# Reordering the opening of a fused Mamba, MLP and mixture-of-experts kernel on one core: when blocks are normalised, when their router logits are made, and when the scan begins

## The chip, the cores and the metric

The kernel runs on one core of one Trainium2 chip. A core has a matrix engine (TensorE, PE in the profile, with its weight loads as PEld), VectorE (DVE), ScalarE (ACT), GpSimd (POOL) and SyncE (SP), which here issues nearly all direct transfers. Each engine works its own list of instructions in the order in which the program names them. The metric is device time in microseconds; before the change it is 1587.38 us (median of three runs, 1585.76 to 1589.98).

## The reference

The input is x, 4096 tokens (2 sequences of 2048) of 256 channels. Cut to what matters:

```
xn = layernorm(x)
# branch s: a Mamba block, then an MLP, each with a residual
r  = rmsnorm(xn)
xp, z = split(r @ in_proj.T)                  # 512 channels each
xc = silu(conv4(xp) + conv_b)
dt, B, C = from xc @ x_proj.T                 # dt = softplus(. @ dt_proj.T + b); 16 states
h_t = h_(t-1) * exp(dt_t * A) + dt_t * xc_t * B_t      # 512 channels x 16 states
y  = (sum_state h_t * C_t + xc * D) * silu(z)
x1 = xn + y @ out_proj.T
s  = x1 + silu(rmsnorm(x1) @ mlp_w1.T) @ mlp_w2.T
# branch g: 8 experts, the best 2 of each token
w  = softmax(xn @ gate_w + gate_b); top 2
g  = silu(sum over the 2 of  w * (relu(xn @ w1[e]) @ w2[e]))
out = x + s * g
```

## The kernel before

Tokens are cut into 8 blocks of 512 (NBLK); a block is four tiles of 128 tokens (J), and blocks are gated in pairs (GB is 2, four groups). The work falls into an opening, a long scan loop and a short ending.

**The opening** (lines 1099 to 1155). For a block b, `moments(b)` takes mean and variance of its four tiles on VectorE (L247, L248). `factors(b0, b1)` turns them into scales and offsets for a range of blocks in one go, 16 small VectorE instructions and four ScalarE ones that alternate (L253 to L265, L234, L235). `norm(b)` has ScalarE write the doubly normalised tile xr (L274) and TensorE transpose it into two PSUM banks (L288): the pair of `ps_b` for an even block, the banks "du" and "y" for an odd one, and for blocks 6 and 7 (EARLY is 6) two of the three banks "h". `logits(b)` copies the transposes to SBUF as xrT (L295), stores xrT (L299), makes router logits on TensorE (L302), and then, in the same function, turns x into its layer norm in place on ScalarE (L309) and stores it (L315). `gate(g)` picks the best two experts for two blocks: some 15 VectorE instructions (L399 to L421), two counting products on TensorE (L415, L418), and 13 more on VectorE (L422 to L438). `scatter_group(g)` then has GpSimd write the rows of those two blocks to the lists of their experts in DRAM: 16 indirect transfers (L456), each a full layer-normed tile. In between stands `front(0)`, a generator: four channel projections of block 0 (L554) with convolution taps on VectorE (L579) and SiLU (L593), the small projection (L599), and the steps dt (L618, `exps` L626 to L632, `log_v` L640, sums L645 and L646). `go(n)` advances it by n pieces. `load_bc` fetches B or C of one pair of states from DRAM, spread over all partitions (L695, 512 KB each). B and C tiles lie in the places in which the opening keeps x (blocks 0 to 5, tags B0 to B5) and xrT (blocks 2 to 7, tags C2 to C7), so a load waits for the last reader of what lies there, and SyncE's later transfers wait behind it.

**The order of evictions.** A product is put on TensorE at once, but the work on its result is put in a list, `later`, with a due time; `tick()` in the opening, and every half step of the scan, moves the time by one and issues what is due.

**The scan loop** (L1311) has 256 steps n: 8 blocks, 4 channel groups d, 8 pairs g of states. A step is one product on VectorE (L1334) and two scans (L1338), with two exponentials on ScalarE (L1228) issued LEAD (2) steps ahead; GpSimd multiplies by C (L1269) and from step 8 on adds the pair (L1271), and TensorE sums over states (L1241) LAG (3) steps later. After each half step, `draw` issues about 2 us of other TensorE work (HALF), each piece counted at the price that its generator yields, from the first list that has some: `pre`, `zs` (gate projections, L705), `projs` (output projections, L759), `chain` (the rest of `front(0)`, then `front(c+1)`), and `side`, all the feed-forward work: 39 expert tiles of 256 tokens, then 16 MLP tiles, each 64 TensorE instructions (L851, L863). A generator that yields "wait" gives up its turn for that half step. `side` is passed over while `pre` holds anything.

`pre` is `routed()`: for blocks 6 and 7 `norm`, `logits` and the last two loads of C; then `gate(3)`, 16 scatters four at a time, `tiles_of_experts()` (a table of which expert owns which tile, some 25 VectorE instructions, L483 to L531), `fill_up()` (eight transfers, L537), and the loads of the first expert. In `side`, the first expert waits four more half steps and then is transposed (L841). Counted out by these rules, the transposes of the first expert tile stand in the program at the first half of step 9.

Of the kernel before, what the change touches and what calls it, by code (L numbers as in the profile page):

```python
# [10 lines left out]
AF = mybir.ActivationFunctionType  # L11
ALU = mybir.AluOpType
# [37 lines left out]
def kernel(  # L50
# [58 lines left out]
    def x_of(b, j):  # L109
        per = J // len(xts[b])  # L110
        return xts[b][j // per][:, j % per, :]
# [128 lines left out]

    stat = rows.tile([P, 8, NI], F32, tag="x1", name="stat")
    mv = stat[:, 0:2, :].rearrange("p a i -> p (a i)").rearrange("p (i a) -> p i a", a=2)
    pts, banks_of = {}, {}
    def moments(b):
        st = hpool.tile([P, J, nc.vector.BN_STATS_DIM], F32, tag="hid", name=f"st{b}")
        for j in range(J):
            nc.vector.bn_stats(st[:, j, :], x_of(b, j))  # L247
            nc.vector.bn_aggr(mv[:, b * J + j, :], st[:, j, :])  # L248

    def factors(b0, b1):  # L250
        i = slice(b0 * J, b1 * J)
        var, rstd, tmp0, ms, r_all, off = (stat[:, 2 + n, i] for n in range(6))
        nc.vector.tensor_scalar_add(var, mv[:, i, 1], LN_EPS)  # L253
        rsqrt(rstd, var, tmp0)

        nc.vector.tensor_mul(ms, rstd, rstd)
        nc.vector.tensor_mul(ms, ms, mv[:, i, 1])
        nc.vector.tensor_scalar_add(ms, ms, RMS_EPS)
        rsqrt(r_all, ms, tmp0)
        nc.vector.tensor_mul(unr[:, i], ms, r_all)  # L260

        nc.vector.tensor_mul(tmp0, rstd, r_all)
        nc.vector.scalar_tensor_tensor(off, mv[:, i, 0], -1.0, tmp0, ALU.mult, ALU.mult)

        nc.vector.scalar_tensor_tensor(var, mv[:, i, 0], -1.0, rstd, ALU.mult, ALU.mult)  # L265
# [4 lines left out]
    def norm(b):  # L270
        xr = work.tile([P, J, DM], F32, tag="h", name=f"xr{b}")
        for j in range(J):
            i = b * J + j
            nc.scalar.activation(  # L274
                xr[:, j, :], x_of(b, j), AF.Identity,
                scale=both_norms[:, i : i + 1], bias=off[:, i : i + 1],
            )
        if b >= EARLY:
            pt, ns = zip(*(bank("h", [P, T], f"pt{b}_{k}") for k in range(KM)))
            banks_of[b] = ns  # L280
        elif b % 2:
            pt = [ps_1.tile([P, T], F32, tag=tag, name=f"pt{b}_{tag}") for tag in ("du", "y")]
        else:
            both = ps_b.tile([P, KM, T], F32, tag="b", name=f"pt{b}")
            pt = [both[:, k, :] for k in range(KM)]
        for k in range(KM):
            for j in range(J):
                nc.tensor.transpose(pt[k][:, ts(j, P)], xr[:, j, ts(k, P)], ident)  # L288
        pts[b] = pt

    def logits(b):
        pool, tag = (bcp, f"C{b}") if b > 1 else (rows, "xrT")
        xrT[b] = pool.tile([P, KM, T], F32, tag=tag, name=f"xrT{b}")
        for k in range(KM):
            nc.scalar.copy(xrT[b][:, k, :], pts[b][k])  # L295
            if b in banks_of:
                drop(*banks_of[b][k])
        if b > 1:
            nc.sync.dma_start(xrd[b], xrT[b])  # L299
        for j in range(J):  # L300
            for k in range(KM):
                nc.tensor.matmul(  # L302
                    lgp[:, b * J + j, :], xrT[b][:, k, ts(j, P)], gw_sb[:, k, :],
                    start=(k == 0), stop=(k == KM - 1),
                )

        for j in range(J):
            i = b * J + j
            nc.scalar.activation(  # L309
                x_of(b, j), x_of(b, j), AF.Identity,  # L310
                scale=rstd[:, i : i + 1], bias=moff[:, i : i + 1],
            )
        per = J // len(xts[b])
        for k, xn in enumerate(xts[b]):
            nc.sync.dma_start(xnd[b][:, ts(k, per), :], xn)  # L315
# [47 lines left out]
    def drop(tag, n):  # L363
        gone.setdefault(tag, set()).add(n)
# [11 lines left out]
    def bank(tag, shape, name):  # L376
        n = ring(tag, 3 if tag == "h" else 1)
        pool = ps_h if tag == "h" else ps_1
        return pool.tile(shape, F32, tag=tag, name=name), n
# [717 lines left out]
        later.run()  # L1097

    later.at_once = False
    for b in range(GB):  # L1100
        moments(b)
    factors(0, GB)
    for b in range(GB):
        norm(b)
        for a in range(GB + 3 * b, GB + 3 * (b + 1)):
            moments(a)
    for b in range(GB):
        logits(b)
    ffns = [Expert(i) for i in range(NTILE)] + [
        Mlp(c, hf) for c in range(NBLK) for hf in range(2)  # L1110
    ]
# [2 lines left out]
    def go(pieces):  # L1114

        for _ in range(pieces):
            next(first)

    go(1)
    go(3)  # L1120
    go(3)
    tick()
    factors(GB, NBLK)
    gate(0)
    scatter_group(0)
    tick()
    norm(2)
    go(3)
    norm(3)
    tick()  # L1130
    logits(2)
    logits(3)
    tick()
    gate(1)
    scatter_group(1)
    tick()
    norm(4)
    go(3)
    tick()
    norm(5)  # L1140
    logits(4)
    go(3)
    tick()
    logits(5)
    tick()
    go(4)
    tick()
    gate(2)
    scatter_group(2)
    assert 0 in bcd and (0, 1) in dt_made  # L1150
    for which, gs in (
        ("B", (0, 1, 6, 7)), ("C", (0, 1)), ("B", (2, 3)), ("C", (2, 3)), ("B", (4, 5)), ("C", (4, 5)),
    ):
        for g in gs:
            load_bc(0, g, which)

    def routed():

        for b in range(EARLY, NBLK):
            norm(b)  # L1160
            yield 4 * MM
            yield "wait"
            logits(b)
            load_bc(0, b, "C")
            yield 2 * MM
            yield "wait"
        gate(NBLK // GB - 1)
        yield "wait"
        for i in range(NI - GI, NI):
            for k in range(TOPK):  # L1170
                scatter(i, k)
            if i % 2:
                yield "wait"
        tiles_of_experts()
        fill_up()
        ffns[0].begin()
        for h in range(4):
            ffns[0].load_w1(h)
            ffns[0].load_w2(h)
        yield "wait"  # L1180
        probabilities()
        for _ in ffns[0].rows():
            pass
# [118 lines left out]
    HALF = 2.0  # L1302

    pre.append(routed())
    chain.append(first)
    side.append(all_ffn(None))
    for n in range(LEAD):
        for q in range(2):
# [1 line left out]
    owed = 0.0  # L1310
    for n in range(NS):  # L1311
        c, d, g = at[n]
        if d == 0 and g == 0 and c % CPB != CPB - 1:
            hs[c] = small.tile([P, ND, DS], F32, tag="hs", name=f"hs{c}")
        if d == 0 and g == 1:
            zs.extend(gate_z(c, k) for k in range(ND))
        if c + 1 < NBLK:
            if d == 0 and g == 1 and c:
                xrT[c + 1] = rows.tile([P, KM, T], F32, tag="xrT", name=f"xrTr{c + 1}")
                nc.sync.dma_start(xrT[c + 1], xrd[c + 1])  # L1320
            if d == 0 and g == (4 if c else 0):
                chain.append(front(c + 1))
        if c > 0 and d == 0 and g == 0:
            projs.append(out_proj(c - 1))
        for q in range(2):
            later.now += 1
            if q == 0:
                if g == 0:
                    assert (c, d) in dt_made
                    dus[c, d] = ps_1.tile([P, T], F32, tag="du", name=f"du{c}_{d}")  # L1330
                    nc.vector.tensor_tensor(dus[c, d], dts[c, d], xcs[c, d], ALU.mult)
                hts[n] = work.tile([P, 2, T], F32, tag="h", name=f"h{c}_{d}_{g}")
                inp = ps_b.tile([P, 2, T], F32, tag="b", name=f"b{c}_{d}_{g}")
                nc.vector.tensor_tensor(  # L1334
                    inp, dus[c, d].unsqueeze(1).to_broadcast([P, 2, T]),
                    bct[c, "B", g], ALU.mult,
                )
            nc.vector.tensor_tensor_scan(  # L1338
                hts[n][:, q, :], das[n][:, q, :], inp[:, q, :],
                0.0 if c % CPB == 0 else hs[c - 1][:, d, 2 * g + q : 2 * g + q + 1],  # L1340
                ALU.mult, ALU.add,
            )
            if q == 0 and n > 0:
                save(n - 1)
                times_c(n - 1)
            exps(n + LEAD, q)
            later.run()
            if q == 0 and n >= LAG:
                sums(n - LAG)
            if q == 0:  # L1350

                past = n - BACK
                if past >= 0 and at[past][1] == ND - 1 and at[past][0] + 1 < NBLK:
                    load_bc(at[past][0] + 1, at[past][2])
            owed = draw(HALF + owed)
# [67 lines left out]
```

## Time and profile before

| | before |
|---|---|
| median of three runs | 1587.38 us |
| the profiled execution's own time | 1574.88 us |
| its span, first to last instruction | 1573.2 us |
| first scan of the loop starts | 113.8 us |
| transposes of the first expert tile start | 192.2 us |
| last scan ends | 1513.6 us |
| busy over the span: PE, DVE, POOL, ACT | 1400.0, 1247.0, 1154.7, 924.3 us |

A profile row of a timeline reads: start, length, engine, line of the kernel, operation, written tile <- read tiles, shapes, and in brackets how long the engine sat idle before it and what released it. Rows with the same line that follow one another are merged (x4 means four of them). Rows of the view by stretches give, for each stretch of time, the busy time of PE, PEld, DVE, ACT and POOL with the number of instructions, then the granted TensorE clock (1.00 is full), the share of the DMA engines and GB/s. A busy PE at half clock does half the work.

### The profile page before, as it was taken

The numbers are of one execution on the slowest core, as the hardware profiler recorded it, in microseconds if no ns is written. First come the engines' busy times: TensorE is split into PE (matmuls) and PEld (weight loads), VectorE is DVE, ScalarE is ACT, GpSimd is POOL, SyncE is SP. The second block draws the span as 40 slices with busy tenths as digits, with TensorE's granted clock in tenths as the row PEclk, the third lists the DMA queues.
The fourth block names the chain that finished last, engine by engine and source line by source line (L and its number), as shares of the span: only waits on it lengthen the run. The fifth ranks groups of instructions, "written<-read, shape, count | busy, mean of one in ns | idle before, by whom it ended". The sixth has DMA issues, their size and how long they took to land. (4 is left out here: it accounts for less than half of the span.)

```text
span 1573.2 us, 18460 instructions
## 1 busy us (share of the span) xinstructions
PE 1400.0 (89%) x5246; PEld 982.6 (62%) x5246; DVE 1247.0 (79%) x1362; ACT 924.3 (59%) x1898; POOL 1154.7 (73%) x767
## 2 busy tenths in 40 slices
PE   4447499999999899999999999989899988899967
PEld 3324167765777577766776677657665656577736
DVE  5435898789788988799869976996689966899952
ACT  4365476566665776567647765676456764465423
POOL 1446768976887689878976888678966678678842
PEclk9556699999999999999999999999999988999988
DMA  5365534763477245924593459234863337636322
GB/s 178 111 239 194 176 100 141 246 231 99 134 237 268 84 130 179 342 84 132 174 339 89 127 168 333 91 117 132 276 215 95 100 101 246 235 121 192 103 97 84
DMA packets 203749, 265.17 MB, mean 169 GB/s; under 512 B 21744, under 2 KB 174192, under 8 KB 203648
## 3 DMA queue, kind: packets, MB, share of 16 engines
q1 hardware_dynamic: 197504, 247.21, 47.7%
q0 software_dynamic: 6144, 16.79, 3.2%
q8 instruction: 42, 0.69, 0.2%
q14 instruction: 59, 0.48, 0.1%
HBM read 227.50 MB, written 36.44 MB: 168 GB/s over the span
## 5 line engine op out<-in xcount | busy, mean ns | idle before, releaser
L1269 POOL TENSOR_TENSOR h<-h,C 128x1024 f32<-128x1024 f32 x256 | 610.1, 2385 | 211.1 <-ACT hs L1265 173.0
L1338 DVE TENSOR_TENSOR_SCAN h<-da,hs,b 128x512 f32<-128x512 f32 x384 | 478.9, 1271 | 32.9 <-PE y L1241 10.2
L1228 ACT ACTIVATE da<-dt,a_neg 128x512 f32<-128x512 f32 x512 | 359.4, 718 | 35.5 <-DVE h L1338 34.1
L1241 PE MATMUL y<-h,ident 128*128 128x512 f32 x594 | 308.3, 620 | 37.3 <-POOL h L1269 25.3
L1334 DVE TENSOR_TENSOR b<-du,B 128x1024 f32<-128x1024 f32 x256 | 314.8, 1230 | 6.2
L851 PE MATMUL phe<-xsTe,w_e 128*128 128x256 f32 x1248 | 288.4, 383 | 7.1 <-ACT hide L951 5.4
L1271 POOL TENSOR_TENSOR h<-h 128x512 f32<-128x512 f32 x215 | 279.1, 1298 | 16.8
L863 PE MATMUL poe<-w_e,hide 128*128 128x256 f32 x1248 | 289.8, 381 | 0.0
L851 PEld LDWEIGHTS phe<-xsTe,w_e 128*128 128x128 f32 x1248 | 238.6, 192 | 71.3 <-issue 26.3
L863 PEld LDWEIGHTS poe<-w_e,hide 128*128 128x128 f32 x1248 | 236.2, 191 | 66.6 <-issue 35.0
L951 ACT ACTIVATE hide<-phe,b 128x256 f32<-128x256 f32 x312 | 129.3, 469 | 128.8 <-PE phe L851 128.8
L1241 PEld LDWEIGHTS y<-h,ident 128*128 128x128 f32 x594 | 112.1, 197 | 129.6 <-issue 66.5
L1338 DVE TENSOR_TENSOR_SCAN h<-da,b 128x512 f32<-128x512 f32 x128 | 151.3, 1211 | 13.1 <-PE y L1241 3.2
L851 PE MATMUL phm<-xsTm,w_m 128*128 128x256 f32 x512 | 128.5, 406 | 13.9 <-DVE hidm L1012 10.4
L851 PEld LDWEIGHTS phm<-xsTm,w_m 128*128 128x128 f32 x512 | 104.0, 205 | 46.0 <-DVE hidm L1012 14.8
L456 POOL DMA_INDIRECT xs_d<-xt,slot x64 | 63.6, 993 | 88.3 <-issue 78.9
L863 PE MATMUL pom<-w_m,hidm 128*128 128x256 f32 x512 | 117.5, 381 | 1.7 <-DVE xom L1083 1.7
L863 PEld LDWEIGHTS pom<-w_m,hidm 128*128 128x128 f32 x512 | 97.6, 192 | 26.1 <-issue 10.3
L1039 POOL DMA_INDIRECT ykm<-ys_d,row_y x64 | 61.9, 967 | 40.5 <-issue 14.4
L1265 ACT COPY hs<-h 128x2 f32<-128x2 f32 x192 | 36.2, 188 | 94.2 <-DVE h L1338 78.0
L1010 ACT ACTIVATE hidm<-phm 128x512 f32<-128x512 f32 x64 | 37.9, 592 | 75.9 <-PE phm L851 65.5
L1012 DVE SCALAR_TENSOR_TENSOR hidm<-hidm,phm 128x512 f32<-128x512 f32 x64 | 42.8, 671 | 48.7 <-ACT hidm L1010 48.7
(174 smaller groups left out, 1463.2 us busy)
## 6 DMA issues: line engine op xcount, KB each, us to landing
w_e<-in_w SPq DMA_DIRECT2D x312, 256.0 KB
B<-bcd SPq DMA_DIRECT2D x64, 512.0 KB
C<-bcd SPq DMA_DIRECT2D x64, 512.0 KB
w_m<-in_mlp_w1T SPq DMA_DIRECT2D x64, 256.0 KB
w_m<-in_mlp_w2T SPq DMA_DIRECT2D x64, 256.0 KB
xs<-xs_d SPq DMA_DIRECT2D x39, 256.0 KB
ys_d<-ys SPq DMA_DIRECT2D x39, 256.0 KB
b<-in_b SPq DMA_DIRECT2D x39, 128.0 KB
```

Of the source, the lines that this page charges most:

```text
L456: r = nc.gpsimd.indirect_dma_start(out=xs_d, out_offset=bass.IndirectOffsetOnAxis(ap=slot[:, k, i : i + 1], axis=0), in_=x_of(i // J, i % ...
L851: nc.tensor.matmul(ph[:, q, :], self.w1[c0 // 2][:, k, ts(q, P)], self.xT[:, k, :], start=(k == 0), stop=(k == KM - 1),)
L863: nc.tensor.matmul(po[:, j, :], self.hid[c // 2][:, c % 2, ts(j, P)], self.w2[c // 2][:, c % 2, :], start=(c == 0 and j == 0), stop=(c == ...
L951: nc.scalar.activation(hc[:, q, :], ph[:, q, :], AF.Relu, bias=self.b1[:, c0 + q : c0 + q + 1])
L1012: lambda: nc.vector.scalar_tensor_tensor(hc, hc, 1.0, ph, ALU.add, ALU.mult), n
L1039: nc.gpsimd.indirect_dma_start(out=yk[k][:, j, :], out_offset=None, in_=ys_d, in_offset=bass.IndirectOffsetOnAxis(ap=row_y[:, k, i0 + j : ...
L1228: nc.scalar.activation(das[n][:, q, :], dts[c, d], AF.Exp, scale=a_neg[:, d, 2 * g + q : 2 * g + q + 1])
L1241: nc.tensor.matmul(ys[c, d], ident, hts[n][:, q, :], start=False, stop=(g == DS // 2 - 1 and q == nq - 1),)
L1269: nc.gpsimd.tensor_tensor(hts[n], hts[n], bct[c, "C", g], ALU.mult)
L1271: nc.gpsimd.tensor_tensor(hts[n][:, 0, :], hts[n][:, 0, :], hts[n][:, 1, :], ALU.add)
L1334: nc.vector.tensor_tensor(inp, dus[c, d].unsqueeze(1).to_broadcast([P, 2, T]), bct[c, "B", g], ALU.mult,)
L1338: nc.vector.tensor_tensor_scan(hts[n][:, q, :], das[n][:, q, :], inp[:, q, :], 0.0 if c % CPB == 0 else hs[c - 1][:, d, 2 * g + q : 2 * g ...
```

## The change

The change reorders the opening. `factors` is called four times for two blocks each, with `moments` of later blocks spread between. The in-place layer norm is split from `logits` into `layer_norm(b)`, which is called later, and which for blocks 0 and 1 runs on GpSimd. `norm(2)` and three projections of `front(0)` are put ahead of `gate(0)` on TensorE's list, `norm(3)` behind it; likewise later on. Blocks 6 and 7 get `norm` and `logits` in the opening, through the same banks as blocks 0 to 5, and `routed()` keeps only their layer norm, `gate(3)` and what follows. The loads of B and C are issued as B0, B1, B6, B7, all eight C, then B2 to B5. In the scan, the rest of `front(0)` joins `chain` at step 3 instead of the start, and for block 0 the gate projections join at step 4 instead of 1, and `front(1)` at step 4 instead of 0.

```diff
--- before.py
+++ after.py
@@ -240,7 +240,7 @@
 
     stat = rows.tile([P, 8, NI], F32, tag="x1", name="stat")
     mv = stat[:, 0:2, :].rearrange("p a i -> p (a i)").rearrange("p (i a) -> p i a", a=2)
-    pts, banks_of = {}, {}
+    pts = {}
     def moments(b):
         st = hpool.tile([P, J, nc.vector.BN_STATS_DIM], F32, tag="hid", name=f"st{b}")
         for j in range(J):
@@ -275,10 +275,7 @@
                 xr[:, j, :], x_of(b, j), AF.Identity,
                 scale=both_norms[:, i : i + 1], bias=off[:, i : i + 1],
             )
-        if b >= EARLY:
-            pt, ns = zip(*(bank("h", [P, T], f"pt{b}_{k}") for k in range(KM)))
-            banks_of[b] = ns
-        elif b % 2:
+        if b % 2:
             pt = [ps_1.tile([P, T], F32, tag=tag, name=f"pt{b}_{tag}") for tag in ("du", "y")]
         else:
             both = ps_b.tile([P, KM, T], F32, tag="b", name=f"pt{b}")
@@ -293,8 +290,6 @@
         xrT[b] = pool.tile([P, KM, T], F32, tag=tag, name=f"xrT{b}")
         for k in range(KM):
             nc.scalar.copy(xrT[b][:, k, :], pts[b][k])
-            if b in banks_of:
-                drop(*banks_of[b][k])
         if b > 1:
             nc.sync.dma_start(xrd[b], xrT[b])
         for j in range(J):
@@ -304,12 +299,20 @@
                     start=(k == 0), stop=(k == KM - 1),
                 )
 
+    def layer_norm(b):
+
         for j in range(J):
             i = b * J + j
-            nc.scalar.activation(
-                x_of(b, j), x_of(b, j), AF.Identity,
-                scale=rstd[:, i : i + 1], bias=moff[:, i : i + 1],
-            )
+            if b < GB:
+                nc.gpsimd.tensor_scalar(
+                    x_of(b, j), x_of(b, j), rstd[:, i : i + 1], moff[:, i : i + 1],
+                    ALU.mult, ALU.add,
+                )
+            else:
+                nc.scalar.activation(
+                    x_of(b, j), x_of(b, j), AF.Identity,
+                    scale=rstd[:, i : i + 1], bias=moff[:, i : i + 1],
+                )
         per = J // len(xts[b])
         for k, xn in enumerate(xts[b]):
             nc.sync.dma_start(xnd[b][:, ts(k, per), :], xn)
@@ -1097,15 +1100,19 @@
         later.run()
 
     later.at_once = False
-    for b in range(GB):
-        moments(b)
+    moments(0)
+    moments(1)
     factors(0, GB)
-    for b in range(GB):
-        norm(b)
-        for a in range(GB + 3 * b, GB + 3 * (b + 1)):
-            moments(a)
-    for b in range(GB):
-        logits(b)
+    norm(0)
+    moments(2)
+    moments(3)
+    norm(1)
+    logits(0)
+    logits(1)
+    factors(2, 4)
+    moments(4)
+    layer_norm(0)
+    layer_norm(1)
     ffns = [Expert(i) for i in range(NTILE)] + [
         Mlp(c, hf) for c in range(NBLK) for hf in range(2)
     ]
@@ -1116,40 +1123,53 @@
         for _ in range(pieces):
             next(first)
 
+
+    norm(2)
     go(1)
     go(3)
     go(3)
     tick()
-    factors(GB, NBLK)
     gate(0)
     scatter_group(0)
-    tick()
-    norm(2)
-    go(3)
     norm(3)
     tick()
+    moments(5)
+    factors(4, 6)
     logits(2)
+    go(3)
     logits(3)
     tick()
+    layer_norm(2)
+    layer_norm(3)
+    norm(4)
     gate(1)
     scatter_group(1)
     tick()
-    norm(4)
-    go(3)
+    moments(6)
+    moments(7)
+    factors(6, 8)
     tick()
     norm(5)
     logits(4)
     go(3)
-    tick()
     logits(5)
     tick()
-    go(4)
+    layer_norm(4)
+    layer_norm(5)
+    norm(6)
+    go(3)
     tick()
     gate(2)
     scatter_group(2)
+    tick()
+    logits(6)
+    norm(7)
+    go(4)
+    tick()
+    logits(7)
     assert 0 in bcd and (0, 1) in dt_made
     for which, gs in (
-        ("B", (0, 1, 6, 7)), ("C", (0, 1)), ("B", (2, 3)), ("C", (2, 3)), ("B", (4, 5)), ("C", (4, 5)),
+        ("B", (0, 1, 6, 7)), ("C", range(DS // 2)), ("B", (2, 3, 4, 5)),
     ):
         for g in gs:
             load_bc(0, g, which)
@@ -1157,13 +1177,7 @@
     def routed():
 
         for b in range(EARLY, NBLK):
-            norm(b)
-            yield 4 * MM
-            yield "wait"
-            logits(b)
-            load_bc(0, b, "C")
-            yield 2 * MM
-            yield "wait"
+            layer_norm(b)
         gate(NBLK // GB - 1)
         yield "wait"
         for i in range(NI - GI, NI):
@@ -1302,7 +1316,6 @@
     HALF = 2.0
 
     pre.append(routed())
-    chain.append(first)
     side.append(all_ffn(None))
     for n in range(LEAD):
         for q in range(2):
@@ -1310,15 +1323,17 @@
     owed = 0.0
     for n in range(NS):
         c, d, g = at[n]
+        if n == 3:
+            chain.append(first)
         if d == 0 and g == 0 and c % CPB != CPB - 1:
             hs[c] = small.tile([P, ND, DS], F32, tag="hs", name=f"hs{c}")
-        if d == 0 and g == 1:
+        if d == 0 and g == (1 if c else 4):
             zs.extend(gate_z(c, k) for k in range(ND))
         if c + 1 < NBLK:
             if d == 0 and g == 1 and c:
                 xrT[c + 1] = rows.tile([P, KM, T], F32, tag="xrT", name=f"xrTr{c + 1}")
                 nc.sync.dma_start(xrT[c + 1], xrd[c + 1])
-            if d == 0 and g == (4 if c else 0):
+            if d == 0 and g == 4:
                 chain.append(front(c + 1))
         if c > 0 and d == 0 and g == 0:
             projs.append(out_proj(c - 1))
```

## The prediction

> **What bounds the kernel now.** First the page's slices, then the busy time by stages.
>
> ```profile
> PE   4447499999999899999999999989899988899967
> PEclk9556699999999999999999999999999988999988
> ```
>
> ```profile
> 0.00:111.70 111.70, 53.80 (x194) 36.16 (x194) 51.10 (x198) 55.97 (x108) 36.60 (x54) 0.73 0.47 164
> 111.70:192.20 80.50, 46.36 (x107) 21.08 (x105) 58.90 (x95) 39.57 (x80) 58.49 (x46) 0.66 0.58 204
> 192.20:300.00 107.80, 104.02 (x409) 75.17 (x410) 90.68 (x81) 70.90 (x148) 87.78 (x53) 0.98 0.47 144
> 300.00:1112.00 812.00, 790.42 (x3069) 565.52 (x3068) 684.62 (x624) 522.53 (x1100) 656.38 (x402) 0.99 0.54 177
> 1112.00:1400.00 288.00, 256.10 (x898) 174.84 (x897) 238.83 (x238) 164.43 (x329) 208.89 (x141) 0.92 0.52 173
> 1400.00:1513.60 113.60, 106.31 (x405) 76.13 (x405) 109.84 (x111) 53.50 (x97) 91.78 (x57) 0.96 0.49 155
> ```
>
> From the first expert tile (192.2) to 1112, where the experts end, PE is busy 97% at full clock: it sets the pace. In the MLP stretch nothing is full (PE 89%, DVE 83%); in the last 114 us DVE is (97%). Before 192.2 no engine is full, and PE runs at about half clock for much of it. So a gain in the opening is worth what it brings forward of PE's and DVE's later work.
>
> Next, what holds the first expert back: the timeline at the turns, then SyncE's waits from 95 to 200.
>
> ```profile
> 34.43 0.18 DVE L227 TENSOR_TENSOR stat<-stat 128x24 f32<-128x24 f32 x1 [8.35 <-ACT stat L235]
> ...
> 45.94 1.22 POOL L456 DMA_INDIRECT xs_d<-xt,slot  x1 [37.31 <-issue]
> ...
> 111.78 1.47 POOL L456 DMA_INDIRECT xs_d<-xt,slot  x1 [15.27 <-issue]
> ...
> 113.78 2.33 DVE L1338 TENSOR_TENSOR_SCAN h<-da,b 128x512 f32<-128x512 f32 x2
> ```
>
> ```profile
> SPq L536 <- DVE scratch L485: 20.0, 1, 20.0
> SPq L934 <- DMA xs_d<-xt,slot: 3.2, 1, 3.2
> ```
>
> The first row is DVE held inside `factors(2,8)`; SyncE stands 20 us for the expert table (L536), then for the last scatters (L934). The chain is router logits, gate, scatters (16 at 1.28 us, 20.5 us a group), the expert table, the rows. `gate(0)` starts at 37.8 because DVE waited 8.35 us for ScalarE inside the one big `factors`; `gate(3)` starts at 143.5, woven into the scan; its last scatter ends at 184.2; the rows land and are transposed 8.0 us later. That chain, not the scan, sets 192.2.
>
> **The opening after the change**, each engine in its order, with durations from before: four norms or layer norms on ACT 2.1, two copies 1.1, 16 logits 2.3 (3.6 cold), three projections 8.1, one 3.4, gate 3.7 + counts 1.3 + 3.0, one tap 0.75, one block's moments 2.1, a `factors` 3.9.
>
> *Blocks 0 to 3.* `factors(2,4)` follows the copies of `logits(1)` and ends at 22.9 if alone. Beside it now run eight layer norms on GpSimd. The trace has only 128x128 there (0.594) and 128x64 (0.39), so 128x256 is about 1.0, 8 us in all from 15 on: inside GpSimd's 37.3 us of idle, so free on GpSimd itself. For DVE this row speaks first:
>
> ```profile
> L402 DVE TENSOR_TENSOR halves<-halves,gb_sb x4: 224/226/2349, 38.1 to 143.8; 128x64 f32<-128x64 f32 x4
> ```
>
> The 2.349 is the one that began beside a 2.35 us GpSimd product. The Trainium skill, "SBUF — State Buffer", section "Who interferes with whom", gives the rule: a VectorE instruction with two SBUF inputs and a GpSimd one that reads SBUF exclude each other for a whole instruction. Without it `factors(2,4)` ends at 22.9; by it, with three or four GpSimd instructions in its last 3 us, at up to 26. Each us here moves the first expert by one, so the sum ends 1.5 better by the first and 1.6 worse by the second; I take 24.4. Then `norm(2)`, transposes and three projections on PE to 35, and only then the counts of `gate(0)`, whose first half was done at 29: they wait 6 us in PE's order, and `taps` behind them on DVE too. Second half done 39.3, so group 0 scatters from 39.4 (45.9 before).
>
> DVE then does nine taps, `moments(5)`, `factors(4,6)`, to 52. ACT stands behind the last: `logits(2)` copies only at 51, though its transposes were ready at 27. PE: logits, the fourth projection, logits, to 59.7. `gate(1)`, whose counts stand behind `norm(4)`'s transposes (ACT: layer norms 2 and 3 first), is done at 69.3; group 1 from 69.4 (76.3).
>
> *Blocks 4 to 7.* DVE: taps, `moments(6)`, `(7)`, `factors(6,8)` to 80. ACT waits again, so SiLU ends at 81.9 instead of 61.7. From there: `norm(5)` 84, copies 86, small projection 92 and its copy 92.8 (80.9 before), layer norms 4, 5 and `norm(6)` 99, the dt exponentials 101.8 to 109.6 (88.8 to 96.5), copies of `logits(6)`, `norm(7)`, `log_v` to 115.2 (101.9), copies of `logits(7)` to 116.4. `gate(2)`'s counts come behind the dt products, at 103; group 2 from 107.4 to 127.9 (111.8).
>
> The loads of B stand behind the store of block 7's xrT on SyncE: from 116.9 instead of 102.6. B0 lands near 120.5, so **the first scan is at 122, 8 us later than before** (the latter waited for `gate(2)` on DVE).
>
> *Into the scan.* `gate(3)` is now drawn in step 0: DVE from 123 to 131, 20 us earlier. Its 16 scatters follow in four lots between the first multiplications by C (2.4 each): 131 + 20.5 + 4.8 = 156.3; plus the 8.0 of before: **first expert at 164.3, 28 us earlier.** A second path has the same end. B2 is now the thirteenth load. Before, ten loads (5.2 MB) landed in some 16 us:
>
> ```profile
> 114.00:116.00 2.00, 0.00 (x0) 0.00 (x0) 2.00 (x2) 0.00 (x0) 1.50 (x2) 0.50 1.05 406
> ```
>
> At 1.6 us each B2 lands at 138; step 2 ends at 142, and the table is drawn behind it. Before, from the table's first row (168.7) to the last expert load took 17.3 us: 159, when the rows are due too. There is no slack for a later B2.
>
> **What 28 us are worth.** Counted out by the lists, the first expert's transposes stand at step 6 instead of 9. PE work that now follows them: twelve products of y at 0.43 (5.2) and two projections of block 1 (3.4), so PE is ahead by 28 - 8.6 = 19.4. DVE has done 9 steps by the count of L1338 at 192, and would have done 5.6 at 164: it owes 3.4 more steps of 3.8 and 6.9 of taps, so it is ahead by 28 - 20 = 8. Gate projections (6.9) go into PE's idle time ahead of the expert in both. Were PE alone the bound, 11 us would come at once, and the feed-forward work would lead the scan by 8.6 us; that pays at the end, where steps with it take 6.0 (63 by L1338 from 1112 to 1490) and steps without 3.85:
>
> ```profile
> 1507.34 2.45 DVE L1338 TENSOR_TENSOR_SCAN h<-da,hs,b 128x512 f32<-128x512 f32 x2
> ...
> 1511.19 2.45 DVE L1338 TENSOR_TENSOR_SCAN h<-da,hs,b 128x512 f32<-128x512 f32 x2
> ```
>
> 0.6 of an MLP tile is 2.8 steps, at 2.15 us: 6. So the ends are 8 (DVE) and 17 (PE). I take **10**, near the DVE end: DVE is 84% busy even where PE is full, and 97% at the end. Profiled execution 1574.88 - 10 = 1565, span 1563; on the median, 1587.38 - 10 = **1577.4**. The median lies 12.5 above the profiled execution; I subtract the same amount from it.
>
> Costed at nothing: B and C of block 0 land before use but for B0 and B2; `front(1)` starting at step 4, since its dt is needed at step 30; the later gate projections, needed from step 10; the banks of blocks 6 and 7, inside the 116.4 above.
>
> **Rivals.**
>
> *ScalarE takes it back (same).* In steps 3 to 8 ACT must do its exponentials (9.8), the second dt pair (6.7 + 1.2), four table loads (5.1), gates (4.1), expert ReLUs (4.2), widening (3): 34 us for six steps, 5.7 a step against 4.5. For it: ACT works in order. Against: it waits idle during the table (10 us) and can take the dt pair there. Price 1.2 x 6 = 7 of the DVE lead of 8: 1586.
>
> *B2 comes late (slower).* The place is SyncE's list: all eight C stand ahead of B2 to B5. At the kernel's mean of 169 GB/s instead of some 330, thirteen loads take 40 us, B2 lands at 157, and table, loads and rows come 19 us later; since step 2 is held as long, the scan loses what the expert loses. The first expert comes at 183 but with step 6 as far away as in the forecast, so 10 - 19 = -9: 1596. It turns to a loss once B2 lands past 148. Against: the row at 406 GB/s is of these very loads.
>
> *PE alone is the bound (faster still).* 17 to 19: 1569. For it: PE's 97% over 920 us. Against: DVE's 97% at the end.
>
> *The router isn't earlier.* If `factors(2,4)` and the waits of ACT for DVE cost as much as the split saves, `gate(3)` would still be 10 us earlier by leaving the weave, and the scan 8 later: about 1587, counted with "same".
>
> **How the numbers follow.** Forecast 0.48, PE alone 0.12, same 0.20, slower 0.20. About 0.3% (4.8 us) is what a measurement of this kernel can tell from no change: faster is below 1582.6, so faster 0.60, same 0.20, slower 0.20. The forecast's own range is 1569 to 1583. The 80% range takes in PE alone and "same" and part of "slower", where nothing caps the loss: 1564 to 1596.
>
> **What would show it.** First scatter near 39, second group 69, third 107; ACT idle about 10 us ahead of the copies of `logits(2)` and of SiLU; first scan at 122; DVE idle ahead of step 2's product until about 138; last scatter of group 3 near 156; first expert transposes near 164; PE full from there; last scan 10 us earlier, with some eight steps of 3.9 at the end. It is wrong if the first expert comes after 172, or comes at 164 and the last scan is not earlier: then a later engine, not the router, paces the kernel.

## The result, and the profile after

The changed kernel takes 1602.17 us (median of four runs, 1600.57 to 1602.69), the kernel before 1586.57 beside it: ratio 1.0094, 95% interval 1.0075 to 1.0112. It is slower by 15.6 us, where 10 us of gain were forecast. Its profiled execution took 1601.96, like its runs. That of the kernel before (1574.88) lies 12.5 below its own median, so the two traces differ by 27 us; the sum below is made on the traces.

First the page's slices of the changed kernel.

```profile
PE   5363899999899999999999999999898988899767
PEclk9555899999999999999999999999999989899978
```

The fifth slice of TensorE is 8 where it was 4, so TensorE fills earlier; but near the end it is emptier, the third slice from the right 7 where it was 9. Next the stretches of the kernel before, then of the changed kernel, cut at the first expert's transposes, step 240 of the scan and the last step (columns as in the prediction: length, then busy time of PE, PEld, DVE, ACT, POOL).

```profile
0.00:192.20 192.20, 100.17 (x299) 57.24 (x299) 110.00 (x291) 95.54 (x188) 95.08 (x100) 0.70 0.51 181
192.20:1431.90 1239.70, 1182.43 (x4504) 839.83 (x4505) 1045.36 (x976) 776.08 (x1611) 980.00 (x612) 0.98 0.53 173
1431.90:1511.20 79.30, 73.14 (x272) 51.07 (x270) 76.20 (x77) 35.28 (x63) 63.76 (x39) 0.96 0.47 153
1511.20:1573.20 62.00, 44.21 (x174) 34.48 (x174) 15.40 (x21) 17.43 (x36) 15.88 (x18) 0.86 0.18 55
```

```profile
0.00:180.10 180.10, 91.20 (x278) 56.06 (x279) 97.35 (x311) 83.02 (x167) 89.40 (x103) 0.67 0.54 193
180.10:1462.30 1282.20, 1208.69 (x4596) 856.30 (x4595) 1067.91 (x995) 793.06 (x1648) 995.85 (x624) 0.98 0.53 170
1462.30:1536.20 73.90, 59.31 (x202) 39.39 (x200) 71.70 (x70) 28.28 (x49) 55.27 (x33) 0.88 0.38 119
1536.20:1600.30 64.10, 44.87 (x174) 35.26 (x174) 15.36 (x21) 17.42 (x36) 15.82 (x18) 0.86 0.18 53
```

Read them as time = TensorE's busy time + its idle time, since it has about the same 1400 us to do in both (1400.0 and 1404.1). Idle is length minus the first busy column: 92.0, 57.3, 6.2, 17.8 before; 88.9, 73.5, 14.6, 19.2 after. So the 27.1 us are -3.1 (opening), +16.2 (middle), +8.4 (steps 240 to 255), +1.4 (tail) and +4.1 of busy time. The first expert comes 12.1 us earlier, but 9.0 of these are work that TensorE had done by then before (100.2 against 91.2). The loss lies behind the edited places, in the scan's later steps.

The turns of the opening, by the timeline of the changed kernel, and two rows that answer the prediction's: the table's wait on SyncE, and the layer norms on GpSimd (nanoseconds: shortest, median, longest).

```profile
37.28 1.25 POOL L459 DMA_INDIRECT xs_d<-xt,slot  x1 [19.06 <-DVE scratch L441]
...
111.77 1.46 POOL L459 DMA_INDIRECT xs_d<-xt,slot  x1 [19.75 <-ACT ex L629]
...
127.82 1.22 DVE L1353 TENSOR_TENSOR_SCAN h<-da,b 128x512 f32<-128x512 f32 x1
...
134.97 0.22 DVE L402 TENSOR_TENSOR halves<-bank_lg,unr 128x64 f32<-128x64 f32 x1 [5.93 <-remote]
...
142.66 0.97 POOL L459 DMA_INDIRECT xs_d<-xt,slot  x1 [10.01 <-issue]
```

```profile
SPq L539 <- DVE scratch L489: 5.1, 1, 5.1
```

```profile
L307 POOL TENSOR_SCALAR xt<-xt,stat x8: 553/559/567, 13.9 to 17.7; 128x256 f32<-128x256 f32 x8
```

The first group scatters 9 us earlier, the third at the same time as before (111.77 against 111.78), the last 11 us earlier (142.66 against 153.96); the first scan comes 14 us later (127.82 against 113.78).

### The profile page after: what moved, and what is told of

Its sections match the earlier page's. It is cut to its first block, busy times and chain, and to the rows that moved or that the text cites. A ratio compares the mean times of both kernels' runs of the same rounds, so it can differ in the third digit from the quotient of the medians.

```text
span 1600.3 us, 18516 instructions
## 1 busy us (share of the span) xinstructions
PE 1404.1 (88%) x5246; PEld 987.0 (62%) x5246; DVE 1252.3 (78%) x1394; ACT 921.8 (58%) x1898; POOL 1156.3 (72%) x775
## 5 line engine op out<-in xcount | busy, mean ns | idle before, releaser
L1353 DVE TENSOR_TENSOR_SCAN h<-da,hs,b 128x512 f32<-128x512 f32 x384 | 479.6, 1271 | 43.1 <-PE y L1255 17.8
L1353 DVE TENSOR_TENSOR_SCAN h<-da,b 128x512 f32<-128x512 f32 x128 | 151.2, 1210 | 11.2 <-PE y L1255 3.2
L854 PE MATMUL phm<-xsTm,w_m 128*128 128x256 f32 x512 | 130.7, 409 | 22.8 <-DVE hidm L1015 19.8
L854 PEld LDWEIGHTS phm<-xsTm,w_m 128*128 128x128 f32 x512 | 103.7, 205 | 55.8 <-DVE hidm L1015 24.9
L582 DVE SCALAR_TENSOR_TENSOR xc<-px,par_sb,xc 128x512 f32<-128x512 f32 x96 | 71.5, 746 | 19.6 <-ACT xc L574 14.9
```

What stands on the lines that cost most here:

```text
L582: nc.vector.scalar_tensor_tensor(v[:, s : s + T], px, conv_w[:, d, KC - 1 - s : KC - s], v[:, s : s + T], ALU.mult, ALU.add,)
L854: nc.tensor.matmul(ph[:, q, :], self.w1[c0 // 2][:, k, ts(q, P)], self.xT[:, k, :], start=(k == 0), stop=(k == KM - 1),)
L1353: nc.vector.tensor_tensor_scan(hts[n][:, q, :], das[n][:, q, :], inp[:, q, :], 0.0 if c % CPB == 0 else hs[c - 1][:, d, 2 * g + q : 2 * g ...
```

## The experiments

Every group of runs was on one chip, beside the kernel before. The chips differ: in the groups of `b_again`, `a_again_2` and `l_only_2`, as in the first comparison, the kernel before takes 1581 to 1587; in those of `a_hold` and `l_half`, 1566 to 1567. I call them late and prompt chips, for a reason told at the end. The changed kernel itself ran on late chips only. Ratios are to the kernel before of the same group.

By *lead* I mean how many expert tiles of feed-forward work stand ahead, in TensorE's list, of a given sum over states, compared with the kernel before. In the changed kernel it is half a tile, because its first expert stands at step 6 instead of 9. The first suspicion (PACE) was that this alone pushes the scan back.

**First group (prompt chip).** `a_hold` takes the lead away and nothing else:

```diff
-                    for _ in range(4):
+                    for _ in range(4 if n else 10):
                         yield "wait"
```

> The changed kernel, with the first expert's transposes held back from step 6 to step 9 of the scan, where the kernel before has them; everything of the opening stays. By TensorE's list the feed-forward work of the changed kernel stands 0.50 of an expert tile ahead of the kernel before at each step (32.0 tiles against 31.5 at the sum number 160); here the lead is 0. Theory PACE: TensorE is full from the first expert to the last, so half a tile of lead (0.5 x 24 us = 12 us) pushes every later scan step back by 12 us, and the end is the scan's end plus a tail; then this kernel gives about 10 to 12 back: about 1591 (1588 to 1594). Theory LATE START (the first scan at 127.8 instead of 113.8 is what is lost): no change, about 1602. Theory CROWDING (gates, front(1) and the dt pair crowded into steps 3 to 8 cost 6 us): no change or a little better, 1600 to 1602.

`a_half` sets HALF from 2.0 to 1.97 in the changed kernel:

> The changed kernel, with the share of other work drawn after each half step at 1.97 instead of 2.0 us. By TensorE's list the lead of the feed-forward work over the kernel before shrinks from 0.50 of a tile at sum 16 to 0.25 at 128, -0.1 at 160 and -0.4 at 256. Theory PACE: the scan's lag of 25 us at the end shrinks by about the lead lost, 0.5 to 0.9 tile x 24 = 12 to 20 us, and the last tiles still fit ahead of the last scan: about 1589 (1585 to 1594). LATE START and CROWDING: 1602, unchanged.

`a_draws` undoes the scan's draws:

```diff
-        if n == 3:
-            chain.append(first)
-        if d == 0 and g == (1 if c else 4):
+        if d == 0 and g == 1:
-            if d == 0 and g == 4:
+            if d == 0 and g == (4 if c else 0):
```

(and `chain.append(first)` ahead of the loop)

> The changed kernel, with the scan's own draws where the kernel before has them: the rest of front(0) from the start, block 0's gate projections at step 1, front(1) at step 0. The first expert's transposes then stand one step earlier still, and the lead of the feed-forward work over the kernel before is 1.0 tile instead of 0.5. CROWDING: steps 3 to 8 lose their crowd, about 6 us come back: 1596. PACE: half a tile more of lead costs 8 to 12 us more: about 1611 (1606 to 1615). LATE START: 1602.

`b_half` sets HALF from 2.0 to 2.04 in the kernel before:

> The kernel before, untouched in the opening, with the share of other work drawn after each half step at 2.04 instead of 2.0 us: the feed-forward work leads the kernel before's own by 0.4 of a tile at sum 64, 0.75 at 128, 1.1 at 192 and 1.5 at 256. PACE: the scan falls behind by up to 24 to 36 us towards the end and gets some 8 us back in steps without feed-forward work: about 1605 (1598 to 1612). LATE START and CROWDING: nothing of theirs is touched, 1587 (1584 to 1590).

| | us | ratio, interval | idle, first expert to step 240 | idle, 240 to 255 |
|---|---|---|---|---|
| a_hold, lead 0 | 1575.82 | 1.0049 (1.0032 to 1.0067) | 60.6 | 7.0 |
| a_half, lead 0.5 to -0.4 | 1588.34 | 1.0137 (1.0117 to 1.0158) | 74.7 | 10.1 |
| a_draws, lead 1.0 | 1575.07 | 1.0054 (1.0034 to 1.0074) | 60.8 | 17.2 |
| b_half, lead 0 to 1.5 | 1581.56 | 1.0088 (1.0066 to 1.0110) | 65.9 | 21.3 |

PACE fails twice: `a_half`, whose lead sinks below nothing, is 12.5 us slower than `a_hold` with no lead, and a whole tile (`a_draws`) costs nothing against none. `b_half` does lie in PACE's range (1598 to 1612 against 1587 are 1.007 to 1.016). It shows a loss with the opening untouched, so LATE START and CROWDING, which gave it none, can't be all of it. CROWDING's 1596 for `a_draws` (1.0057) is met in number, but `a_hold`, which keeps most of the crowd, is as fast. PACE's end is visible too: idle time after step 240 is 7 without a lead, 17 with a whole tile and 21 with one and a half (10 in `a_half`, 0.4 behind by then). In every kernel here 53 of the 55 tiles are done when the last scan begins; the last two need that scan, so feed-forward work done earlier cannot shorten the end. The middle column groups otherwise: no lead or a whole tile about 61, a lead that drifts 66 to 75. That suggested FIT: what matters is where inside a tile each scan step falls, and a whole tile puts every step back in the same place.

**Second group (late chip): the two halves of the change.**

> The kernel before, unchanged, for a trace from the same chip as the experiments beside it. In its first trace the gate of the second group began at 68.6 after 13.9 us of idle VectorE, 10.4 us after its router logits were done (58.2), with 'remote' as the releaser; in b_half, whose opening is the same, it began with the end of the logits (59.0) and everything behind it came 10 us earlier. Theory HICCUP (those 10 us belong to single executions, not to the program): here the gate of the second group is at 59, the first scan near 103, the first expert's transposes near 178, about 1567 on a chip as fast as the last. Rival: the 10 us are the program's own on most executions: 68.6, 113.8 and 192.

> The changed kernel, unchanged, beside the kernel before on one chip. HICCUP: second gate at 58, the first scan near 124 (20 us after the kernel before's, not 14), first expert near 175 (3 us before it, not 12), and the time 0.9 to 1.3% above the kernel before. Rival: 127.8 and 180 as in its first trace, 12 us ahead of the kernel before's first expert.

`o_only` is the kernel before with the new order up to block 5, and blocks 6 and 7, the draws and the order of loads as before. Against the changed kernel, in the opening:

```diff
-    layer_norm(5)
-    norm(6)
+    layer_norm(5)
     go(3)
...
-    logits(6)
-    norm(7)
     go(4)
     tick()
-    logits(7)
```

> The kernel before with the first half of the change alone: factors by two blocks, the layer norms behind the logits (blocks 0 and 1 on GpSimd), norm(2) and the first projection ahead of the counts. The norms and logits of blocks 6 and 7 stay in the scan, the draws and the order of loads too, and the first expert stands at step 9 of the scan as before. Theory QUEUES (ScalarE stands inside the later factors waiting for VectorE, so SiLU and dt come late): first scatter at 36 instead of 46, second gate still near 58, SiLU of the last channels and dt some 8 to 12 us later, first scan near 113 instead of 103, 1570 to 1574 where the kernel before has 1567. Rival FORECAST (an earlier router is worth its us): first expert 5 or more us earlier and 1560 to 1565.

`l_only` is the kernel before with blocks 6 and 7 ahead of the scan, through the banks of the other blocks, with only the loads of C left of them in `routed()`, and its first expert held at step 9:

```diff
     gate(2)
     scatter_group(2)
+    tick()
+    norm(6)
+    logits(6)
+    norm(7)
+    tick()
+    logits(7)
```

> The kernel before with the second half of the change alone: norm and logits of blocks 6 and 7 behind the third gate in the opening, through the banks of the other blocks, and the last router gate at the head of the scan; factors, layer norms, counts and draws as before, and the first expert held at step 9. Theory QUEUES: the first scan comes later by what stands ahead of it, some 8 us (111 instead of 103); the last gate near 115 instead of 131, its scatters from 122; the time within 3 us of the kernel before, 1564 to 1570, since the first expert waits for TensorE's order. Rival LATE START (each us of a later first scan is lost): 1573 to 1577.

`b_again` shows the second gate at 68.5, the first scan at 115.1 and the first expert at 195.8: not a hiccup of one execution, as I had taken it. `a_again`: first scan 127.0, first expert 178.8, ratio 1.0123 (1.0090 to 1.0155). `o_only`: 0.9996 (0.9984 to 1.0009). Its first scatter is at 37.0 and its third group at 105.7 instead of 113.1, but the last gate, drawn in the scan, starts at 146.0 (147.2 in `b_again`), and the first expert comes at 194.6. Neither QUEUES (slower) nor FORECAST (faster) holds: seven us won ahead of the scan are down to one at the last gate. `l_only`: 0.9961 (0.9945 to 0.9976), though its first scan is 11 us late (126.2); the last gate starts at 127.3 and the first expert comes at 186.4, both earlier. LATE START is out.

**Third group (prompt chip): half a tile against a whole one.** `l_half` and `l_one` are `l_only` with 8 and 4 half steps of wait instead of 12; `a_lag` is `a_hold` with 14 instead of 10.

> l_only with its first expert held until step 7 instead of 9: the feed-forward work then leads the kernel before by about half a tile (32.0 tiles against 31.5 at sum 160), as in the changed kernel; the opening is that of l_only. Theory LEAD (the half tile is what the changed kernel loses by, not its opening): the idle time of TensorE between steps 16 and 240 rises from 59 to some 70 us and after step 240 from 7 to 14, the last scan comes 15 to 20 us later than in l_only, ratio to the kernel before 1.006 to 1.010 on a chip where l_only has 0.996. Rival OPENING (the changed kernel's own opening is to blame): ratio 0.995 to 0.998.

> l_only without any hold: the first expert stands at step 5 and the feed-forward work leads by a whole tile (32.5 against 31.5 at sum 160). Theory PACE (each us of lead is a us of lag for the scan, and what comes back at the end is less): worse than l_half, ratio 1.010 to 1.016. Theory FIT (it is not how far ahead, but where in a tile each scan step falls; a whole tile puts every step back where the kernel before has it): idle time between 16 and 240 back at about 60, after 240 some 17, the opening 5 us better; ratio 0.996 to 1.000, far below l_half.

> The changed kernel with its first expert held until step 11: the feed-forward work lags the kernel before's list by half a tile (31.0 against 31.5 at sum 160). PACE: the scan gains, the tiles still end within the last scan steps: the same as a_hold or some us better, a_hold - 3. FIT: half a tile off, idle time between 16 and 240 above 68 again: 6 to 12 us slower than a_hold.

> a_hold once more (the changed kernel, its first expert at step 9), beside the others of this group. In its first run the kernel before was on a chip on which its second gate didn't wait for the scatters, and a_hold had 1.005. If TensorE's signals come late here (second gate of the kernel before near 68), the opening of the changed kernel is worth what it is in l_only: ratio 0.994 to 0.998; where they come at once, 1.005 again.

`l_half` has 1587.95, ratio 1.0152 (1.0134 to 1.0170); `l_one` 1566.67, ratio 1.0006 (0.9996 to 1.0015). Up to step 6 the two traces agree within 0.2 us; a wait of two steps ahead of one tile then makes 21 us. (LEAD's 1.006 to 1.010 was meant for a chip where `l_only` has 0.996; `l_only` was not run on a prompt chip.) Their stretches (middle, steps 240 to 255), `l_half` first:

```profile
169.40:1447.30 1277.90, 1202.74 (x4583) 855.00 (x4582) 1061.02 (x987) 784.51 (x1631) 990.76 (x621) 0.98 0.53 171
1447.30:1521.20 73.90, 59.53 (x202) 39.46 (x200) 71.49 (x69) 28.28 (x49) 55.24 (x33) 0.88 0.38 119
```

```profile
165.80:1426.40 1260.60, 1198.16 (x4589) 850.30 (x4588) 1060.37 (x991) 786.79 (x1637) 991.81 (x620) 0.98 0.53 173
1426.40:1501.30 74.90, 58.04 (x205) 38.67 (x202) 70.34 (x68) 29.63 (x51) 57.39 (x34) 0.89 0.37 116
```

Idle in the middle is 75.2 against 62.4, though the opening is the same and the whole tile leads by more: FIT holds, PACE doesn't. Idle time isn't all of the 21.9 us between these traces: 10.0 are busy time of TensorE (1403.4 against 1393.4), which FIT says nothing of. The granted clock matters for busy time (in the changed kernel's opening sixteen router products took 3.64 us at 0.50 and 1.95 at 1.00), and it was 0.937 against 0.941 in these two executions. But over all runs its median is 0.942 for both kernels while their times stay 21 us apart, so a lower clock is not the cause. `a_hold_2` has 1.0059 (1.0037 to 1.0080), as `a_hold`; `a_lag` 1.0111 (1.0091 to 1.0132), 8.3 us above it, with 73.5 us idle in the middle against 64.3.

**Fourth group (late chip): the changed kernel itself.** `b_lag` is the kernel before with 8 half steps of wait instead of 4. `c1d` is `a_draws` with `moments(5)` and `factors(4, 6)` moved from ahead of `logits(2)` to behind `scatter_group(1)`, `norm(4)` behind them, and `factors(6, 8)` moved behind `layer_norm(5)`.

> The changed kernel, unchanged, on one chip with a_hold_3. FIT (half a tile of lead costs): 12 to 20 us above a_hold_3; where TensorE's signals are prompt, ratio to the kernel before about 1.015 to 1.018; where they are late, about 1.010 to 1.012. Rival (a_hold only looked better because its chip was another): within 4 us of a_hold_3.

> The changed kernel with its first expert at step 9 (a_hold again), beside the changed kernel. FIT: ratio 1.005 on a chip with prompt signals, 0.995 to 0.998 on one with late signals; 12 to 20 us below the changed kernel on either. Rival: within 4 us of it.

> The kernel before, with nothing changed but four more half steps of wait ahead of its first expert (step 11 instead of 9), so that the feed-forward work lags its own list by half a tile (31.0 against 31.5 at sum 160). FIT: idle time of TensorE between steps 16 and 240 rises from 56 to 68 or more; with the later expert (4 to 6 us more idle ahead of it) the ratio is 1.008 to 1.014. Rival (a half tile hurts only with the new opening): only the later expert shows, ratio 1.002 to 1.004.

> a_draws (changed kernel, draws as before, a whole tile of lead) with factors(4,6) and moments(5) moved behind the second gate, and factors(6,8) behind the logits of block 5, so that ScalarE's copies of block 2 and the SiLU don't stand behind them. Theory QUEUES: second gate some 8 to 12 us earlier (46 to 50), SiLU near 70, the first scan near 112 instead of 124, first expert's transposes near 166 instead of 174, the time 5 to 10 us below a_draws: ratio 0.998 to 1.001 where a_draws has 1.0054. Rival: the scans' start follows the third gate and the loads of B; nothing moves by over 3 us, 1.004 to 1.007.

On one chip the changed kernel has 1600.78 (1.0092, 1.0068 to 1.0116) and `a_hold_3` 1579.51 (0.9963, 0.9951 to 0.9975): **21.3 us apart, and with the lead taken away the change is faster than the kernel before.** That is a little more than the 12 to 20 that FIT expected. Their traces agree within 0.6 us up to step 8, and the median granted clock of their runs is the same to 0.002 (0.934 and 0.935). The middle and the steps after 240, `a_again_2` first:

```profile
180.70:1463.20 1282.50, 1208.79 (x4596) 856.38 (x4595) 1068.52 (x995) 792.60 (x1648) 995.52 (x624) 0.98 0.52 170
1463.20:1537.10 73.90, 59.29 (x202) 39.44 (x200) 71.78 (x70) 28.27 (x49) 55.23 (x33) 0.88 0.37 119
```

```profile
191.00:1434.40 1243.40, 1181.75 (x4504) 839.33 (x4503) 1049.04 (x979) 776.16 (x1611) 978.92 (x611) 0.98 0.53 173
1434.40:1513.80 79.40, 73.27 (x273) 51.17 (x271) 76.94 (x77) 35.26 (x64) 64.51 (x40) 0.96 0.48 153
```

Idle: 73.7 against 61.7, and 14.6 against 6.1. TensorE's waits in the middle (us in total, times, longest), `a_again_2` and then `a_hold_3`:

```profile
PE phe L854 <- ACT hide L954: 8.8, 3, 4.5
PE pxsm L844 <- ACT xrm L1005: 7.4, 3, 5.8
...
PE phm L854 <- DVE h L1353: 5.4, 1, 5.4
...
PE phm L854 <- DVE sz L1263: 4.8, 1, 4.8
```

```profile
PE phe L854 <- ACT hide L954: 5.4, 2, 4.5
...
PE pxsm L844 <- ACT xrm L1005: 4.9, 2, 3.9
```

There is no one wait: a few more single ones of 2 to 6 us, and one group goes the other way (`phm` for VectorE's `hidm`: 7.2 against 11.6). The rows of `h` and `sz` are waits for VectorE's work for the scan; that the others too come from the scan's work in the way is a reading, not shown. Which pair of pieces must not meet was not tried.

`b_lag`: 1.0040 (1.0024 to 1.0056), with 70.5 us idle in the middle instead of 55.8 in `b_again` (on another late chip): a half tile costs idle time in the kernel before too. The idle time is as FIT had it, the ratio as the rival, since the busy time is 5.9 shorter by the traces; a tile that is late, not early, adds only 2.0 after step 240 (8.2). So half a tile late costs 5.2 us here and 8.3 in `a_lag`, half a tile early 21.3 twice. `c1d`: 1.0078 (1.0055 to 1.0101), a miss. The second gate did come at 49.6. But then `moments(5)` and `factors(4, 6)`, now beside the second group's scatters, took VectorE 21.8 us; in the changed kernel, beside the first group's, they took 6.4. Their first and last rows, `c1d` with two of the gaps first, then the changed kernel:

```profile
57.70 0.41 DVE L247 BATCH_NORM_STATS2 st<-xt 128x6 f32<-128x256 f32 x1
60.94 0.18 DVE L248 BATCH_NORM_AGGREGATE stat<-st 128x2 f32<-128x6 f32 x1 [2.83 <-remote]
...
75.08 0.24 DVE L229 TENSOR_SCALAR stat<-stat 128x8 f32<-128x8 f32 x1 [1.25 <-DVE stat L228]
...
79.38 0.16 DVE L265 SCALAR_TENSOR_TENSOR stat<-stat 128x8 f32<-128x8 f32 x1
```

```profile
43.75 0.42 DVE L247 BATCH_NORM_STATS2 st<-xt 128x6 f32<-128x256 f32 x1
...
49.98 0.16 DVE L265 SCALAR_TENSOR_TENSOR stat<-stat 128x8 f32<-128x8 f32 x1
```

The instructions are as short as before; the time lies in gaps ahead of them, most of them where VectorE needs only its own results. ScalarE stood 17.5 us for `moments(5)`, SiLU began at 84.1 instead of near 70, later VectorE stood 18.3 us inside `factors(6, 8)` for ScalarE, and the first scan came at 137.7. So `c1d` doesn't tell what its order would be worth without these gaps. Behind the opening it bears FIT out: with its whole tile of lead it idles 62.3 us in the middle.

**Last two (late chip).**

> l_only again (logits of blocks 6 and 7 ahead of the scan, all else as before, first expert at step 9), beside l_one. Where TensorE's signals come late during the scatters (kernel before near 1582 to 1587): ratio 0.995 to 0.997 as before; where they are prompt (near 1567): 1.002 to 1.006, as a_hold.

> l_one again (the same without the hold, first expert at step 5, a whole tile of lead), beside l_only_2. FIT: 2 to 7 us below l_only_2, by the idle time that it saves ahead of the first expert: 0.991 to 0.995 where signals are late, 1.000 to 1.001 where they are prompt. PACE: 7 or more us above l_only_2.

`l_only_2`: 1575.80, 0.9952 (0.9930 to 0.9975). `l_one_2`: 1578.97, 0.9962 (0.9948 to 0.9975). A whole tile is neither better nor measurably worse than none; the 2 to 7 us that I expected of it did not come (11.2 us more idle after step 240 by the traces, against 4.3 less up to the first expert). Both beat the kernel before and the changed one on this chip; `l_one`, which ran on both kinds, is level with the kernel before on the prompt chip (1.0006).

## Why the prediction was wrong

- **What 28 us are worth** is the step that failed. It let the feed-forward work run ahead of the scan and put that down as a gain, of 6 us at the end. 5.4 of the 6 came: steps 240 to 255 take 73.9 instead of 79.3. But with half a tile of lead the scan had fallen 30 us behind by step 240, and it never got the rest back: its last step starts 25.0 us late (1536.2 against 1511.2). In place of that gain the lead costs 21.3 by the medians (`a_again_2` less `a_hold_3`). By their traces it is 25.4: 12.0 of idle in the middle, 8.5 after step 240, 1.4 in the tail, 5.8 of busy time, less 2.3 in the opening. The busy time stays open; traces of one kernel differ by as much (1407.1 in `a_hold`, 1399.2 in `a_hold_2`). The forecast's two bounds, TensorE ahead by 19.4 and VectorE by 8, both assumed that work stays packed when two streams shift against each other; the idle time that the shift adds has no place in them.
- **The opening's worth** comes near the forecast on the late chips: with the lead away, 6.8 us (`a_hold_3`), where 10 were forecast. That nearness is luck: the first expert, held at step 9, comes there at 191.0, 1 to 5 us ahead of the kernel before (192.2 and 195.8 in two traces), not 28. On the prompt chips the same opening loses 0.5 to 0.6%.
- **The first expert** came at 180.1, not 164.3. Scatters first at 37.3 (39.4 forecast), second group 71.9 (69.4), third 111.8 (107.4). SiLU 84.5 (81.9) and dt 106.2 (101.8) put the loads of B at 122.8 (116.9) and the first scan at 127.8 (122). Then 5.9 us that no step of mine had: `gate(3)` had its logits done at 123.7 but VectorE began it only at 134.97, after standing idle, so it ended at 142.6 instead of 131. Its scatters took 24.9 (25.3 forecast), to 167.5. From there 12.6 instead of 8.0: gate projections and sums of the scan stand ahead of the transposes in TensorE's list. By my own rule (wrong if it comes after 172) the forecast fell here too.
- **TensorE's lead** of 19.4 was 28 less 8.6 of moved work. The moved work was right (9.0); the rest is 12.1 - 9.0 = 3.1.
- **Rivals.** B2 was not late: VectorE waited for a load of B only ahead of the first scan (4.3 us). ScalarE's crowd in steps 3 to 8, but for the expert's own pieces, is in `a_hold_3` too, which is faster than before; and `l_half` loses the 21 us with the draws as before. So the crowd isn't the cause. "The router isn't earlier" is what `o_only` shows of the first half of the change. A loss was forecast at 0.20, but by another mechanism; 1602 lies above the range.
- **The rule on shared access** ("SBUF — State Buffer", section "Who interferes with whom", in the Trainium skill) was not put to the test: the layer norms took 0.56 us each, not the 1.0 that I estimated, and the last began at 17.7, so they were over before the products with two inputs in `factors(2,4)` began at 19.6; that ended at 22.8. The 1.5 us that I allowed for it were not needed.

## What to carry to other kernels

Where an engine is full and two streams share it in a fixed order, time is its work plus its idle time: ask of a change to the opening how much idle it removes, and not how much earlier a milestone comes. An edit that lets one stream start earlier can also shift it against the other for the whole loop, as here; hold the start back to its old place, and to a whole tile from it, before you judge the edit. A stream whose last pieces wait for the other's last step gained nothing by leading here.

## What the runs showed of the hardware

On some chips VectorE started late on results that were ready, while GpSimd's scatters ran. The same opening, `b_again` (late chip) and then `b_half` (prompt chip):

```profile
56.78 2.19 PE L302 MATMUL bank_lg<-gw_sb,xrT 128*128 128x8 f32 x13
...
65.30 0.97 POOL L456 DMA_INDIRECT xs_d<-xt,slot  x1 [0.30 <-issue]
68.55 0.23 DVE L399 TENSOR_TENSOR halves<-bank_lg,unr 128x64 f32<-128x64 f32 x1 [13.48 <-remote]
```

```profile
56.76 2.19 PE L302 MATMUL bank_lg<-gw_sb,xrT 128*128 128x8 f32 x12
...
58.99 0.22 DVE L399 TENSOR_TENSOR halves<-bank_lg,unr 128x64 f32<-128x64 f32 x1 [4.06 <-PE bank_lg L302]
```

The logits end at 59.0 in both; the gate waits for them alone, and starts 0.0 us later on one chip, 9.6 us later on the other, 2.3 us after the last scatter of the group. In the changed kernel the last gate waits in the same way (134.97, scatters to 132.7), and on the prompt chip doesn't (125.9 in `a_hold`). It need not last to the end of a group: in `c1d` the second gate starts at 49.6, 4.3 us after its logits, amid the scatters. Nor is it only TensorE's signal: the gaps in `c1d` above stand ahead of instructions that wait for VectorE itself. With the late gate the first expert of the kernel before comes at 195.8; without it, in `b_half`, at 177.6. The same program takes 1581 to 1587 us on late chips and 1566 to 1567 on prompt ones. The kernel before was not traced on a prompt chip, but two programs were traced on both kinds: the first expert of `l_one` comes at 165.8 or 180.5, and its times lie 12.3 us apart; with `a_hold` it comes at 183.4 to 185.1 or 191.0, and the times lie 4 to 6 apart. Both idle in the middle about alike on either kind, so the opening makes most of the difference. Why VectorE starts late was not found out. It decides the sign of small changes: with the lead away, the opening of the changed kernel gains 0.4% on a late chip (`a_hold_3`), where the kernel before loses those 10 us, and costs 0.5% on a prompt one (`a_hold`).
